# Attention 1 of a graph network: 20 destination blocks instead of 16 leave the gathers, the windows are sought before the table, and the run table comes in as an input

## The chip, the core and the metric

The kernel runs on one core of a Trainium2 chip. The metric is device time in microseconds (us) for one execution. The kernel before takes 4396.92 us, the median of three runs (4395.07 to 4397.64).

The core has five engines that run side by side, each from its own in-order queue: PE (matmul; PEld is its weight load), DVE (vector), ACT (scalar, activation), POOL (GpSimd) and SP (it only issues DMAs here). DMAs are issued from the queues of SP, ACT and POOL. Gathers of table rows by index (indirect DMAs) are issued from POOL's queue. SBUF is the working memory of 128 partitions, PSUM holds matmul results, and tensors named `dram` lie in HBM.

## The reference, cut to what matters

Input are 6250 nodes of 128 features and 200000 edges `src -> dst`, sorted by `dst`. Two graph layers follow each other, each behind a layer norm and a ReLU, each added to its input:

```
h = relu(layernorm(x))
x = x + gat(gat(h, 4 heads of 16).elu(), 1 head of 128)   # attention 1, attention 2
h = relu(layernorm(x))
x = x + conv(h)                                           # edge MLP, messages, scatter-add

gat: feat = x @ W;  el, er = (feat * attn_l).sum, (feat * attn_r).sum
     e = leaky_relu(el[src] + er[dst]);  alpha = softmax of e over the edges of one dst
     out[dst] = sum of alpha * feat[src]
```

The change lies in attention 1: for each destination node, the softmax-weighted sum of the features of its edges' sources, with four heads.

## The kernel before, in words

Nodes are taken in NB = 49 blocks of 128. The program has four stages: a head (layer norm, features, the table), attention 1, attention 2, and the convolution.

**Head.** `x` is loaded in seven pieces. `norm_stats` (L289) makes mean and variance of a block. The loop at L574 takes four blocks at a time: ReLU of the normed rows on ACT (L579), transposes on PE, an eviction on DVE (L314), a matmul with the weights (L591), and evictions into `t1` (L593) and `er1` (L594). `t1` is written to the HBM tensor `table1` in four parts (L600): 76 words a node, being features, `el` and two exponentials of it. Beside this, the first edge of each block is sought in the sorted `dst` (L205 to L241): compare with the first entry of segments of 40, sum the counts by matmul, fetch one segment a block, and count in it. `write_runs` (L258) writes a table `runs` of overlapping runs of 128 edges (`src` and `dst` as 16-bit words, one run every 16 edges).

**Attention 1, gathered blocks.** NG = 49 - DENSE1 = 33 blocks are gathered. A window of 34 x 128 edges is loaded for each. The edges come in five groups (8, 8, 8, 8 and 2 tiles of 128 edges, `GROUPS`). `gather` (L317) issues one indirect DMA a tile, so 34 a block, into one of six buffers `G`. `attend` (L353) makes a one-hot of the destinations (L324), the node factors by matmul (L360 to L366), the messages (L367), splits them in two halves (L331, L332), and adds them up by matmul (L377). `load_low` (L342) loads, for each block, the low bits of `dst` to all partitions (`oht`, 1088 KB), and `node_hot` (L350) makes a one-hot of it. `finish1` (L793) ends four blocks: division by the sums, ELU, and the rows for attention 2.

**Counts.** Attention 2, and the dense blocks of attention 1, need for each pair of source and destination node how many edges join them. These counts are made for all 49 blocks, in 196 steps of a quarter block. A window of two destination nodes holds at most 128 edges. `seek_windows` (L710) looks for the first edge of each window, 25 chunks of 128 windows: a first search by compares and matmuls stands at L617 to L627; then, for each chunk, one indirect fetch of a segment of 160 entries (L715) and a count in it (L720, L721). `fetch_run` (L729) fetches the runs by index, `cut_windows` (L736) turns them to keys, and `count` (L764) compares them with all slots (two instructions at L773), multiplies (L784), casts on ACT (L786), and writes the counts to HBM (L788).

**Attention 1, dense blocks.** The last DENSE1 = 16 blocks are not gathered. `dense1` (L852) takes four blocks at a time, in two passes of two heads, and runs over all 49 source blocks in seven steps of seven: load counts and factors (L861, L864), a steep ReLU on ACT that says for each pair of nodes on which side of the leaky ReLU it lies (L892), its minimum with the counts on DVE (L895, one instruction for each of two heads, 112 in all), and matmuls (L902, L908). `fill_rhs1` (L684) makes the factors from the table in seven steps, each with multiplications and splits at L694 to L705.

**Order.** The loop at L1003 goes over the gathered blocks and their groups. It mixes in count steps and dense steps by how far it has come: count steps from block LAG = 3, dense steps from block LAG_D = 7, both spread to the end of the last gathered block (L1027, L1030). The fetches of the segments (L715) go between the gathers of the first two blocks and the rest at the start of the third, the fills stand in the second and third. A framework orders the instructions of each engine around this and sets the semaphores; `keep` fixes the order of those that are wrapped in it. After the loop, flags are made (miscounts, overflow) and branched on, and attention 2 begins.

**Attention 2** takes two blocks at a time over all 49 source blocks: counts loaded, a ramp on ACT (L1188), two instructions on DVE (L1192, L1193), matmuls (L1197). **The convolution** takes the edges in 1563 tiles with one gather each.

Of the kernel before, what the change touches and what calls it, by code (L numbers as in the profile page):

```python
# [42 lines left out]
P = 128  # L43
SB = 8
GROUPS = ((0, 8), (8, 8), (16, 8), (24, 8), (32, 2))
K = 34
# [7 lines left out]
LAG = 3  # L54
AHEAD = 4
DENSE1, LAG_D = 16, 7
# [10 lines left out]
def gnn_kernel(ctx: ExitStack, tc: tile.TileContext, x, src, dst, attr4, attr8,  # L67
               W1, al1, ar1, b1, W2, al2, ar2, b2,
               Wl0, Wl1, Ws0, Ws1, Wm1, Wm2, Wtp, Wf0, Wf1, src_t, dst_t, attr4_t, attr8_t, out):
# [23 lines left out]
    NROW = (E - WCAP) // WSTEP + 1  # L93
# [11 lines left out]
    ps_bank = ps_pre.enter_context(tc.tile_pool(name="ps_bank", bufs=2, space=PSUM))  # L105

# [52 lines left out]
    fin = one.enter_context(tc.tile_pool(name="fin1", bufs=1))  # L159
    aw = one.enter_context(tc.tile_pool(name="aw", bufs=2))  # L160
# [3 lines left out]
    df = seek.enter_context(tc.tile_pool(name="df", bufs=1)).tile([GP, ROWT + 1], F32, name="df")  # L164
    listed = ExitStack()
    find = listed.enter_context(tc.tile_pool(name="find", bufs=1))
    both = []
    for name, v in (("di", dst), ("si", src)):
        t = find.tile([GP, ROWT + WCAP], I32, name=name)
        nc.vector.memset(t[:, ROWT:], NB * P)  # L170
        rows = v.rearrange("(p t) -> p t", p=GP)
        nc.sync.dma_start(t[:, :ROWT], rows)
        nc.sync.dma_start(t[:GP - 1, ROWT:], rows[1:, :WCAP])
        both.insert(0, t)

    w1_sb = const.tile([D, HD], F32, name="w1_sb")
    nc.scalar.dma_start(w1_sb, W1)
    load_x()
    w2_sb = const.tile([HD, D], F32, name="w2_sb")
    nc.scalar.dma_start(w2_sb, W2)  # L180
    a1_sb = const.tile([HD, 2 * H1], F32, name="a1_sb")
    nc.vector.memset(a1_sb, 0.0)
    for j, a in ((0, al1), (1, ar1)):
        for h in range(H1):
            nc.scalar.dma_start(a1_sb[h * DH:(h + 1) * DH, j * H1 + h:j * H1 + h + 1],
                                a[h:h + 1, :].rearrange("o d -> d o"))
    a2_sb = const.tile([D, 2], F32, name="a2_sb")
    for j, a in ((0, al2), (1, ar2)):
        nc.scalar.dma_start(a2_sb[:, j:j + 1], a.rearrange("o d -> d o"))
# [5 lines left out]
    wfirst = const.tile([P, NC], I32, name="wfirst")  # L195

    runs = dram.tile([NROW, 2, WCAP], I16, name="runs")
    di = both[1]
    nc.vector.tensor_copy(df, di[:, :ROWT + 1])
    falls = find.tile([GP, ROWT], F32, tag="row", name="falls")  # L200
    nc.vector.tensor_tensor(falls, df[:, :ROWT], df[:, 1:], op=OP.is_gt)
    fall = find.tile([GP, 1], F32, name="fall")
    nc.vector.tensor_reduce(fall, falls, axis=AX.X, op=OP.max)
    NS = ROWT // SEG
    below = find.tile([GP, NB + 1, NS], F32, name="below")  # L205
    nc.vector.tensor_tensor(below, df[:, 0:ROWT:SEG][:, None, :].to_broadcast([GP, NB + 1, NS]),
                            starts[:GP, :, None].to_broadcast([GP, NB + 1, NS]), op=OP.is_lt)
    nbelow = find.tile([GP, NB + 1], F32, name="nbelow")
    nc.vector.tensor_reduce(nbelow, below, axis=AX.X, op=OP.add)
    ps = small()  # L210
    nc.tensor.matmul(ps[:NB + 1, 0:1], nbelow, ones[:GP], start=True, stop=True)
    nc.tensor.matmul(ps[:NB + 1, 1:2], fall.to_broadcast([GP, NB + 1]), ones[:GP], start=True, stop=True)
    seg = find.tile([NB + 1, 1], F32, name="seg")
    nc.vector.tensor_scalar(seg, ps[:NB + 1, 0:1], -1.0, 0.0, op0=OP.add, op1=OP.max)
    seg_i = find.tile([NB + 1, 1], I32, name="seg_i")
    nc.vector.tensor_copy(seg_i, seg)
    part_i = find.tile([NB + 1, SEG], I32, name="part_i")
    nc.gpsimd.indirect_dma_start(
        out=part_i, out_offset=None, in_=dst.rearrange("(s t) -> s t", t=SEG),
        in_offset=bass.IndirectOffsetOnAxis(ap=seg_i[:, 0:1], axis=0))  # L220
    part = find.tile([NB + 1, SEG], F32, name="part")
    nc.vector.tensor_copy(part, part_i)
    nc.vector.tensor_scalar(part, part, own_start[:NB + 1], None, op0=OP.is_lt)
    found = find.tile([NB + 1, 2], F32, name="found")
    nc.vector.tensor_reduce(found[:, 1:2], part, axis=AX.X, op=OP.add)
    nc.vector.scalar_tensor_tensor(found[:, 0:1], seg, float(SEG), found[:, 1:2], op0=OP.mult, op1=OP.add)
    nc.vector.tensor_copy(found[:, 1:2], ps[:NB + 1, 1:2])
    pr = small()
    for j in range(2):
        nc.tensor.matmul(pr[:1, j * P:j * P + NB + 1], found[:, j:j + 1], ident[:NB + 1, :NB + 1],  # L230
                         start=True, stop=True)
    ends = find.tile([1, 2, NB + 1], F32, name="ends")
    nc.vector.tensor_copy(ends, pr[:1, :2 * P].rearrange("o (j b) -> o j b", j=2)[:, :, :NB + 1])
    first = find.tile([1, NB], F32, name="first")
    nc.vector.tensor_scalar(first, ends[:, 0, :NB], float(E - CAP), None, op0=OP.min)
    nc.vector.tensor_copy(first_i, first)
# [9 lines left out]
    for t in both:  # L246
        raw = pool.tile([P, LONG], BF16, tag="row", name="raw", bufs=3)[:GP, :ROWT + WCAP].bitcast(I16)
        nc.scalar.copy(raw, t)
        raws.append(raw)
# [1298 lines left out]
```

## Time and profile before

| what | value |
|---|---|
| runs, median of three | 4396.92 us |
| the profiled execution | 4406.11 us, span 4404.4 us |
| before the first gather of attention 1 | 112.7 us |
| first to last gather of attention 1 | 112.68 to 1778.53 us |
| last gather to the first ramp of attention 2 | 1778.53 to 1849.45 us |
| attention 2, then convolution, to the end | 1849.45 to 4404.4 us |
| busy over the span: PE, DVE, ACT, POOL | 69%, 81%, 62%, 63% |
| mean granted PE clock | 0.832 |

A profile is one execution of the kernel; its times are from the start of its span. The page has, for each engine, the busy share of 40 equal slices of the span as digits (9 is 90% or more). A group of instructions shows the line, the engine, the operation, what is written from what, and how often; then the busy time, the mean length of one in ns, and the idle time of the engine just before them with what ended it. "issue" there means that the engine waited for nothing the profile shows. The timeline lists instructions by start and length. A line of waits reads: who waited for whom, us in total, how many times, the longest. SPq, ACTq are the DMA issues in those queues.

### The profile page before, as it was taken

The numbers are of one execution on the slowest core, as the hardware profiler recorded it, in microseconds if no ns is written. First come the engines' busy times: TensorE is split into PE (matmuls) and PEld (weight loads), VectorE is DVE, ScalarE is ACT, GpSimd is POOL, SyncE is SP. The second block draws the span as 40 slices with busy tenths as digits, with TensorE's granted clock in tenths as the row PEclk, the third lists the DMA queues.
The fourth block names the chain that finished last, engine by engine and source line by source line (L and its number), as shares of the span: only waits on it lengthen the run. The fifth ranks groups of instructions, "written<-read, shape, count | busy, mean of one in ns | idle before, by whom it ended". The sixth has DMA issues, their size and how long they took to land. (4 is left out here: it accounts for less than half of the span.)

```text
span 4404.4 us, 61759 instructions
## 1 busy us (share of the span) xinstructions
PE 3042.9 (69%) x19255; PEld 2147.9 (49%) x19256; DVE 3565.2 (81%) x6184; ACT 2712.6 (62%) x6200; POOL 2795.3 (63%) x2752
## 2 busy tenths in 40 slices
PE   4115665666477566579998677777777777777777
PEld 3115444544355444478887344444444444444444
DVE  5258776788688688688888799999999999899998
ACT  3024556576486577689999565555555555555555
POOL 0777777777777777110000777777777777777775
PEclk9999677677677778699999788888888888888888
DMA  4346464565466556554453222222222222222221
GB/s 109 67 120 171 128 168 129 164 177 158 126 178 165 150 156 169 172 177 167 153 171 107 61 63 63 62 63 64 62 63 63 63 62 63 63 62 63 64 61 51
DMA packets 410029, 484.00 MB, mean 110 GB/s; under 512 B 248457, under 2 KB 296367, under 8 KB 405454
## 3 DMA queue, kind: packets, MB, share of 16 engines
q1 hardware_dynamic: 258854, 239.58, 18.6%
q0 software_dynamic: 87952, 149.96, 15.0%
q10 hardware_dynamic: 62872, 90.28, 5.7%
q8 instruction: 159, 2.61, 0.3%
q14 instruction: 192, 1.57, 0.1%
HBM read 369.70 MB, written 109.82 MB: 109 GB/s over the span
## 5 line engine op out<-in xcount | busy, mean ns | idle before, releaser
L319 POOL DMA_INDIRECT G<-table,srcc x1563 | 1475.1, 944 | 1003.3 <-DVE kept L1239 525.6
L319 POOL DMA_INDIRECT G<-table,srcw x1122 | 1249.0, 1113 | 417.1 <-issue 314.9
L786 ACT CAST ca<-small 128x392 bf16<-128x392 f32 x784 | 350.2, 491 | 335.9 <-PE small L784 307.0
L892 ACT ACTIVATE up<-erb,sel 128x512 bf16<-128x512 f32 x784 | 516.1, 726 | 8.6 <-DMA oht<-dlow 3.6
L1188 ACT ACTIVATE ramp<-erb,sel 128x256 bf16<-128x256 f32 (+1 forms) x1225 | 491.7, 499 | 20.7 <-DVE up L1192 14.4
L1335 PE MATMUL whole<-halves,ohr 128*128 128x512 f32 x1563 | 503.9, 461 | 0.7 <-ACT acc L1365 0.7
L1277 ACT ACTIVATE g<-G,a 128x128 f32<-128x128 f32 x1563 | 481.4, 393 | 2.0 <-DMA G<-table,srcc 0.2
L1270 PEld LDWEIGHTS big<-wtp_sb,hid 64*128 64x128 f32 x3126 | 263.6, 249 | 372.8 <-issue 358.2
L1270 PE MATMUL big<-wtp_sb,hid 64*128 64x128 f32 x3126 | 306.1, 351 | 150.2 <-DVE halves L1324 149.8
L784 PE MATMUL small<-key,lo 128*128 128x98 bf16 x3136 | 299.9, 237 | 139.6 <-ACT ca L786 109.0
L908 PE MATMUL up<-up,rc 128*102 128x512 bf16 x784 | 297.0, 539 | 142.2 <-DVE up L895 141.4
L1335 PEld LDWEIGHTS whole<-halves,ohr 128*128 128x128 f32 x1563 | 316.6, 210 | 129.5 <-issue 54.1
L377 PE MATMUL whole<-halves,ohr 128*128 128x136 f32 x1122 | 240.1, 356 | 174.6 <-DVE halves L332 138.7
L1258 PE MATMUL layer<-hid,wm_sb 128*128 128x512 f32 x392 | 341.1, 969 | 11.9 <-ACT hid L1261 11.1
L1261 ACT ACTIVATE hid<-layer 128x512 f32<-128x512 f32 x392 | 230.8, 589 | 189.6 <-PE layer L1258 189.6
L1258 PE MATMUL layer<-a8t,wm_sb 16*128 16x512 f32 x392 | 230.0, 667 | 157.2 <-ACT hid L1261 148.1
L784 PEld LDWEIGHTS <-lo 128*128 128x128 bf16 x3136 | 228.7, 115 | 209.9 <-issue 175.9
L1315 ACT CAST halves<-mess 128x512 fp32r<-128x512 f32 x195 | 114.4, 587 | 329.7 <-DVE mess L1302 329.7
L1307 DVE TENSOR_TENSOR halves<-mess,halves 128x512 fp32r<-128x512 f32 x391 | 267.8, 685 | 55.3 <-ACT halves L1310 39.8
L377 PEld LDWEIGHTS whole<-halves,ohr 128*128 128x128 f32 x1122 | 204.7, 255 | 194.7 <-DVE halves L332 137.3
L1197 PE MATMUL big<-rhs,up 128*128 128x196 bf16 x2401 | 240.5, 250 | 49.6 <-DVE up L1192 41.6
L773 DVE TENSOR_TENSOR lo<-slots,turned 128x2048 bf16<-128x2048 bf16 x196 | 238.3, 1216 | 37.4 <-PE small L784 37.2
(296 smaller groups left out, 6294.4 us busy)
## 6 DMA issues: line engine op xcount, KB each, us to landing
counts<-ca ACTq DMA_DIRECT2D x196, 392.0 KB
ct<-counts SPq DMA_DIRECT2D x192, 392.0 KB
ctc<-counts SPq DMA_DIRECT2D x896, 56.0 KB
oht<-dlow SPq DMA_DIRECT2D x33, 1088.0 KB
G<-table,srcc POOLq DMA_INDIRECT x1563
rc<-rhs SPq DMA_DIRECT2D x56, 358.8 KB
G<-table,srcw POOLq DMA_INDIRECT x1122
a8t<-attr_rows SPq DMA_DIRECT2D x391, 16.0 KB
```

The source lines that it names most:

```text
L319: nc.gpsimd.indirect_dma_start(out=G[:, c, :], out_offset=None, in_=table, in_offset=bass.IndirectOffsetOnAxis(ap=idx[:, c:c + 1], axis=0))
L377: nc.tensor.matmul(acc, oh[:, c, :], ms[:, c].rearrange("e s f -> e (s f)"), start=start and c == 0, stop=stop and c == n - 1)
L784: nc.tensor.matmul(ps[:, k * NKEY:(k + 1) * NKEY], lo[:, a, :, r], ky[:, a, :, r], start=True, stop=True)
L786: nc.scalar.copy(ca[:, :, i * W:(i + WBANK) * W].rearrange("p h (k d) -> p h k d", d=W), ps[:, :WBANK * NKEY].rearrange("p (k h d) -> p h ...
L892: nc.scalar.activation(up[:, i], erb[:, j], AF.Relu, bias=sel1[:, h0 + i, 2 * q + j:2 * q + j + 1], scale=STEEP)
L908: nc.tensor.matmul(sums["ups"][j][:2 * C1, :], r[:, i, c:c + 2 * C1], up[:, i], start=h0 + i == 0, stop=h0 + i == NB - 1)
L1188: nc.scalar.activation(ramp[:, h, :n * P], erb[:, :n * P], AF.Relu, bias=sel2[:, h0 + h, :], scale=STEEP)
L1258: keep(nc.tensor.matmul(ph, w, x[:, :npr * P], start=True, stop=True))
L1270: keep(nc.tensor.matmul(pw[:, c, :], hid[half, j * P:(j + 1) * P], wtp_sb[half].rearrange("x p u -> x (p u)"), start=True, stop=True))
L1277: keep(nc.scalar.activation(g0[:, c], G[:, c, :], AF.Copy, scale=a0[:, c, :]))
L1307: keep(nc.vector.tensor_tensor(ms[:, cs, 1, 1], m, ms[:, cs, 0, 1], op=OP.subtract))
L1335: keep(nc.tensor.matmul(acc, oh[:, c, :], ms[:, c].rearrange("e s h i u -> e (s h i u)"), start=start, stop=stop))
```

## The change

It does five things.

1. DENSE1 goes from 16 to 20: 29 blocks are gathered, 20 are dense. The dense steps start at block 3 and are due 20 tiles before the end of the last gathered block; the count steps start at block 0 and are due three blocks before it.
2. `runs` is an input of the program in 32-bit words; `write_runs` and the load of `src` for it are gone. So are most small weight loads: `a1_w`, `a2_w`, `lin_w`, `wm1_w`, `wm2_w`, `wtp_w` and `wf_w` come in ready-made and are loaded whole, on SP.
3. The search for the windows goes ahead of the table: the compares (`segments`), the fetches in five groups of five chunks (`fetch_parts`) and the counts in them (`count_parts`).
4. The head is written as a pipeline in a kept order: statistics of eight blocks at a time, `features` in five phases of which each call of `through` advances up to five groups of blocks, with the eviction of the transposes on ACT. The table is written in three parts of 24, 16 and 9 blocks. The check whether `dst` falls (`find_falls`) comes last.
5. The pools `fin1` and `aw` are opened once the memory of the head is released, the fills stand in blocks 0 and 1, and statistics and the windows' shift have a kept order.

```diff
-LAG = 3
 AHEAD = 4
-DENSE1, LAG_D = 16, 7
+DENSE1, LAG_D, AFTER, AFTER_D = 20, 3, 3, 20
...
+    def segments(i0, i1):
+        for i in range(i0, i1):
+            below = find.tile([GP, NC * P], BF16, name="belowc", bufs=2)
+            keep(nc.vector.tensor_scalar(below, wstarts, df[:, i * WSEG:i * WSEG + 1], None, op0=OP.is_gt))
+            for c in range(NC):
+                keep(nc.tensor.matmul(pcount[:, c:c + 1], below[:, c * P:(c + 1) * P], ones_b, start=i + c == 0,
+                                      stop=i == NSEG - 1 and c == NC - 1))
...
+    def fetch_parts(q):
+        part = find.tile([P, NQS, WSEG], I32, name="wpart_i", bufs=2)
+        for j in range(NQS):
+            nc.gpsimd.indirect_dma_start(
+                out=part[:, j, :], out_offset=None, in_=dst.rearrange("(s t) -> s t", t=WSEG),
+                in_offset=bass.IndirectOffsetOnAxis(ap=wseg_i[:, q * NQS + j:q * NQS + j + 1], axis=0))
+        wparts[q] = part
+
+    def count_parts(q):
+        less = find.tile([P, NQS, WSEG], F32, name="wpart")
+        cs = slice(q * NQS, (q + 1) * NQS)
+        keep(nc.vector.tensor_tensor(less, wparts.pop(q), own_w[:, cs, None].to_broadcast([P, NQS, WSEG]), op=OP.is_lt))
+        keep(nc.vector.tensor_reduce(wfound[:, cs], less, axis=AX.X, op=OP.add))
...
+    def through(k):
+        for d in range(5):
+            if 0 <= k - d < len(gens):
+                next(gens[k - d])
+
+    c0 = stats(0)
+    keep(nc.vector.tensor_copy(df, di))
+    deque(c0, 0)
+    c1 = stats(1)
+    through(0)
+    segments(0, 1)
...
+    segments(6, NSEG)
+    window_segments()
+    for q in range(2):
+        fetch_parts(q)
...
+    through(9)
+    write_table(0, 24)
+    through(10)
+    count_parts(1)
+    fetch_parts(3)
+    through(11)
+    through(12)
+    count_parts(2)
+    fetch_parts(4)
+    through(13)
+    write_table(24, 40)
+    through(14)
+    through(15)
+    through(16)
+    write_table(40, NB)
     pq = pool.tile([P, NB, 2 * H1], F32, name="pq")
     node_factors(pq, er1, H1)
     split3(pre, pq3, pq, [P, NB, 2 * H1])
+    for q in range(3, 5):
+        count_parts(q)
+    window_rows()
...
     for b in range(AHEAD):
         load_window(b)
+    for c in chunks[:2]:
+        fetch_run(c)
     for b in range(AHEAD):
         shift_window(b)
     low = load_low(0)
+    tables[chunks[0]] = cut_windows(chunks[0])
     for b in range(NG):
-        if b == LAG - 1:
-            deque(seeking, 0)
-        if b == LAG:
-            tables[chunks[0]] = cut_windows(chunks[0])
...
-            if b < LAG - 1:
-                for _ in range(2):
-                    next(seeking, None)
-            if b + 1 < LAG:
-                write_runs(b * len(GROUPS) + q, (LAG - 1) * len(GROUPS))
-            if b == 1 or b == 2 and q < NB // HS - len(GROUPS):
-                fill_rhs1(((b - 1) * len(GROUPS) + q) * HS, HS)
-            if b == LAG - 1 and q == 3:
-                for c in chunks[:2]:
-                    fetch_run(c)
-            due = len(steps) * ((b - LAG) * K + s + n) // ((NG - LAG) * K)
+            if b == 0 or b == 1 and q < NB // HS - len(GROUPS):
+                fill_rhs1((b * len(GROUPS) + q) * HS, HS)
+            due = min(len(steps), len(steps) * (b * K + s + n) // ((NG - AFTER) * K))
             todo = deque(steps[done:max(done, due)])
             done = max(done, due)
-            due = n_dense * ((b - LAG_D) * K + s + n) // ((NG - LAG_D) * K)
+            due = min(n_dense, n_dense * ((b - LAG_D) * K + s + n) // ((NG - LAG_D) * K - AFTER_D))
             more = max(0, due - taken)
```

## The prediction

> **What bounds the kernel now.** I read the page's slices first. The gathers of attention 1 and of the convolution are the two blocks of POOL work. Attention 1 lasts until about slice 17, and POOL stands at 7 there from slice 2 on.
>
> ```profile
> POOL 0777777777777777110000777777777777777775
> L319 POOL DMA_INDIRECT G<-table,srcw x1122 | 1249.0, 1113 | 417.1 <-issue 314.9
> L892 ACT ACTIVATE up<-erb,sel 128x512 bf16<-128x512 f32 x784 | 516.1, 726 | 8.6 <-DMA oht<-dlow 3.6
> ```
>
> A 7 looks like slack, but the idle time in front of the gathers is "issue": POOL waited for nothing. The timeline shows the step, here with the DVE row that lies under it:
>
> ```profile
> 1762.41 0.94 POOL L319 DMA_INDIRECT G<-table,srcw  x1 [0.30 <-issue]
> 1763.66 0.94 POOL L319 DMA_INDIRECT G<-table,srcw  x1 [0.30 <-issue]
> 1764.33 2.01 DVE L895 TENSOR_TENSOR up<-up,ctc 128x3584 bf16<-128x3584 bf16 x1
> 1764.91 2.25 POOL L319 DMA_INDIRECT G<-table,srcw  x1 [0.30 <-issue]
> 1767.46 0.95 POOL L319 DMA_INDIRECT G<-table,srcw  x1 [0.30 <-issue]
> ```
>
> One gather steps every 1.25 us (0.95 busy, 0.30 issue), back to back, except where a dense min (L895) runs: that gather takes 2.25 instead of 0.94. So POOL is the bound of attention 1 at "78%". The table by stretches gives the others' load:
>
> ```profile
> 112.70:300.00 187.30, 23.56 (x162) 21.84 (x161) 61.19 (x194) 13.39 (x27) 141.58 (x146) 1.00 0.37 85
> 300.00:430.00 130.00, 69.69 (x524) 62.18 (x525) 116.28 (x307) 63.52 (x141) 99.68 (x96) 1.00 0.58 161
> 430.00:1779.00 1349.00, 867.67 (x6052) 627.55 (x6050) 1038.21 (x1829) 865.22 (x1725) 1057.44 (x932) 0.73 0.58 157
> 1779.00:1870.00 91.00, 52.63 (x367) 40.66 (x365) 54.83 (x134) 57.21 (x133) 0.00 (x0) 0.66 0.46 163
> ```
>
> Columns: stretch, length, busy PE, PE loads, DVE, ACT, POOL, clock. DVE is 33% busy in the first stretch and 77% in the third. What DVE waits for, between 600 and 1750 us:
>
> ```profile
> DVE w L364 <- DMA G<-table,srcw: 130.4, 27, 9.1
> DVE lo L773 <- PE small L784: 36.9, 34, 3.0
> DVE h L810 <- PE small L807: 18.1, 8, 3.9
> ```
>
> Most of its idle time is waiting for gathered rows. Last, the two ends of the stage:
>
> ```profile
> 72.70 27.42 SPq L600 DMA_DIRECT2D table<-t  x4
> 112.68 0.96 POOL L319 DMA_INDIRECT G<-table,srcw  x1 [65.17 <-PE pe L360]
> 1777.59 0.94 POOL L319 DMA_INDIRECT G<-table,srcw  x1 [0.30 <-issue]
> 1820.44 0.22 ACT L989 COPY sums<-whole 128x68 f32<-128x68 f32 x1
> 1839.11 0.33 ACTq L788 DMA_DIRECT2D counts<-ca  x1
> 1841.77 0.33 SPq L830 DMA_DIRECT2D rhs2d<-rr  x1
> 1849.45 5.69 ACT L1188 ACTIVATE ramp<-erb,sel 128x256 bf16<-128x256 f32 x14
> ```
>
> The last table write is issued by 100.12, the gathers run from 112.68 to 1778.53 (1665.9 us), then 70.9 us pass until attention 2's first ramp: counts and dense work spread to the last gathered block are still being worked off.
>
> **The change, part by part** (in the profiled execution: 4406.1 us, span 4404.4; it lies 9.2 above the median 4396.9, and I carry the difference over).
>
> *Gathers.* 33 blocks become 29: 4x34 = 136 gathers leave the POOL queue, and the 25 fetches of window segments (L715), which stood between the gathers at the same step (122.69, 123.94), go ahead of the first gather. The 25 run fetches stay. 161 x 1.25 = -201.3 us.
>
> *Mins.* A fifth group of four dense blocks brings 28 mins: 112 become 140. Of the 112, 107 start before the last gather; with the dense work due 20 tiles before the end I count all 140 there, 33 more. Price of one: the gathers cost 212.5/211 = 1.007 us before 430, where no min runs, and 1036.5/913 = 1.135 after. Excess over 0.94 after 430: 178 us, at most 178/107 = 1.66 a min; taking off the earlier background (0.067 each, 61 us) leaves 1.09. Samples: 2.25 - 0.94 = 1.31, and 1.39 at 1771.21. I take 1.3, by the samples: +42.9 (36 to 55). Four fewer node one-hots (L350, 1.37 long) give back about 0.8 each: -3.
>
> The Trainium skill, page "SBUF — State Buffer", section "SBUF: two separate sides", says that a DMA issued by GpSimd cannot write its descriptors while VectorE holds the port pair both share, and then blocks to the end of that instruction. The rows agree: the long gather ends 0.8 us behind its min. By the rule a min could cost up to its whole 2.02 us; 33 of them would be 67 in place of 43.
>
> *Gather stage: -161.*
>
> *Head.* Window segments (ten compares of about 1 us and 250 small matmuls, at 100 to 108 before), five groups of fetches and the blocks' firsts now lie ahead of the table's last write, in a kept order. DVE had 62.9 us busy in the first 112.7; the edit adds about 6 there (counts of parts). The 25 fetches (31 us) lie under POOL's 65.17 us idle; without that cover the last five would cost 6. Gone: the load and cast of src (781 KB), and the run writes (625 KB each) which share the queues with the table's landing between 100.12 and 112.68. In ACT's queue 13 evictions of about 0.6 replace DVE's; ACT had 33.3 busy of 112.7. The first two run fetches stand behind two gathers in POOL's queue and wait for the last counts of parts on DVE, which have falls (1.79 and 1.81) and the factors' split (about 2) in front of them; the other gathers queue behind that wait. It is covered by the table's landing, 12.6, or costs up to 5 of it. That 12.6 can shrink to the 7.6 that a 1088 KB load takes (issued 50.64, used 58.26); kept order on in-order engines can cost as much as the ten compares. I take -6, between -20 and +15. The kept weights' loads move to SP ahead of the windows; nothing waits for them until later.
>
> *Compute beside the gathers.* Counts run from block 0, due three blocks early: 196/26 = 7.54 steps a block (was 196/30 = 6.53); mins 140 over 864 tiles, 5.51 a block (was 112/26 = 4.31). DVE rows: a gathered block 16.5 (four groups of 1.21+0.72+0.68+0.35+0.22+0.18, a small one, the one-hot 1.37), a count step 1.216+0.963 = 2.18, a min 2.02, the rest 4.2. Before: 16.5+14.2+8.7+4.2 = 43.6; measured between 600 and 1750 (790 gathers, 23.2 blocks of 49.5): busy 38.2, waiting for gathered rows 6.0, other waits 5.3. So rows overlap by a factor 0.876. After: 16.5+16.4+11.1+4.6 = 48.6, busy 42.6, other waits 5.9: 48.5 us. POOL's block: 34x1.25 + 1.2 (run) + 5.51x1.3 + 1.5 (the one-hot's 0.8 and small delays) = 52.4. POOL stays the bound, by 3.9 us. ACT by the same scaling 38.5, PE 37.1. Blocks 0 and 1 also hold the seven fills (L694 to L705, 49.5 us of DVE): about 60 a block against POOL's 45, a lag of 30; POOL runs ahead by six buffers of eight tiles, 60 us, which hides it. If that cover is gone the lag falls on the path. I take +10 (0 to 70).
>
> *Tail.* With counts due three blocks and the dense work 20 tiles early, behind the last gather stand: landing 2.5, the last small group 5 (sum of its DVE and ACT rows), finish1 6.5 (1820.44 to 1826.95), flags and branch 11 (1838.48 to 1849.45): 25, and a little lag: 30. 30 - 70.9 = -41 (-11 if DVE is still a block behind).
>
> Attention 2 and the convolution keep their work; the statistics now have a kept order in attention 2 too, hidden behind ACT, which is busy 512.1 of the 530 us from 1870 to 2400 (without that cover, the 12 groups could cost about 1 us each); runs as an input of 32-bit words makes a fetch 1 KB a row, which no row prices, and the fetch is a POOL step like any other (1043 ns against 1113): zero, at most 25x1.
>
> **Sum:** -161 - 6 + 10 - 41 = -198: 4406.1 - 198 = 4208 in the profiled execution, **4199 us** by the median.
>
> **The rivals.**
> - *Compute becomes the bound of the first 26 blocks.* For it: DVE would be 42.6/52.4 = 81% busy there (77% before), PE 71% at a granted clock of 0.73. Against: 1700 to 1800 held DVE at 87.5% and the gathers still stepped on. If the other waits double to 12 a block, a block takes 42.6 + 12 = 54.6: 2.2 more in 26 blocks, 57, and some 10 of lag are left at the tail: about 4265.
> - *The tail stays*: work due early is done late, since every engine queue is in order. +30: 4229.
> - *The mins cost the gathers their whole length*: 33 x 0.7 more, 4222. This is the skill's rule at its end.
> - *Slower.* The node one-hots' load (oht, 1088 KB) stands in SP's queue among 16 loads of counts per dense step; SP waited 309 us there for mins to free buffers. If it is exposed in each block, 29 x 7.6 = 220 come back: 4419. It decides from 7 us a block; between 600 and 1750 DVE waited for it 4.3 us in 23 blocks.
>
> **How the numbers follow.** Forecast 0.52 (its own range 4170 to 4225), compute bound 0.20, tail 0.12, long mins 0.10, slower 0.05, else 0.01. Low end: head -20, mins at 1.09, no drag, tail 25: -235, 4160. High end takes in the compute bound: 4285. Within 0.2% is 8.8 us, about what a measurement can tell from no change; only a near full loss lands there (0.01). Faster 0.94, slower 0.05.
>
> **What would show it.** In the profile after: 986 gathers of about 1.14 to 1.16 us, idle still "issue", none behind DVE; the first near 106, the last near 1610; 30 us to the first ramp; attention 2 and convolution as long as before (2555 us from the first ramp to the end). Wrong if gathers wait for "DVE msg" or "PE pe", if DVE's waits for gathered rows vanish while a block is longer than 53, or if the first gather comes after 125.

## The result, and the profile after

The changed kernel takes 4268.82 us, the median of four runs (4261.89 to 4277.34), against 4397.28 us for the kernel before beside it (four runs, 4395.07 to 4398.40). The ratio is 0.9709, 95% interval 0.969 to 0.9728: 128.5 us faster. The forecast was 4199, so a third of the expected gain did not come, and the time lies close to the rival in which compute becomes the bound (4265).

The profiled execution took 4266.29 us (span 4264.5). Its parts beside those of the kernel before, from the timelines of the two:

| part | before | after | difference | forecast |
|---|---|---|---|---|
| start to the first gather | 112.7 | 114.4 | +1.8 | -6 |
| first to last gather | 1665.9 | 1542.2 | -123.7 | -161 + 10 |
| last gather to the first ramp | 70.9 | 50.4 | -20.5 | -41 |
| first ramp to the end | 2554.9 | 2557.5 | +2.6 | 0 |

The sum is -139.8; the profiled execution of the kernel before lay 9.2 us above its median, that of the changed one 2.5 below.

The stage of the gathers can be taken apart further. A POOL step of 1.25 us (0.94 busy, 0.30 issue) is one unit; what a gather or fetch takes above 0.94 is its excess; a gap between two steps above 0.45 us, less the usual 0.30, is a wait. Issues after the first gather: 1172 became 1011, x 1.25 = -201.3. Excess: 193.4 became 225.1, +31.7. Waits: 10.2 (in 3 gaps) became 55.8 (in 18 gaps), +45.6. Together -124.0, which is the measured -123.7.

The page of the changed kernel, slices and groups:

```profile
POOL 3777777777777774100003777777777777777775
L346 POOL DMA_INDIRECT G<-table,srcw x986 | 1149.5, 1166 | 362.6 <-issue 269.0
...
L945 DVE TENSOR_TENSOR up<-up,ctc 128x3584 bf16<-128x3584 bf16 x140 | 282.8, 2021 | 68.2 <-ACT up L942 56.6
```

The gathers' block of 7s is about one slice shorter, and their mean went from 1113 to 1166 ns, because more of them lie under a min (L945). The mins themselves are as long as before (2021 ns), but 56.6 us of idle time now stand in front of them, waiting for the activations L942 (before, 15.8 us in front of L895).

The two ends of the stage, from the timelines of POOL and ACT, with a step under a min (2.29 us long) between them:

```profile
114.45 0.94 POOL L346 DMA_INDIRECT G<-table,srcw  x1 [6.42 <-PE small L713]
...
1651.87 2.29 POOL L346 DMA_INDIRECT G<-table,srcw  x1 [0.30 <-issue]
...
1655.72 0.94 POOL L346 DMA_INDIRECT G<-table,srcw  x1 [0.30 <-issue]
...
1707.05 1.31 ACT L1228 ACTIVATE ramp<-erb,sel 128x256 bf16<-128x256 f32 x3
```

The step is what it was, 1.25 us, and 2.29 for 0.94 under a min (L945 at 1651.33).

What POOL waited for between the first gather and the last (us in total, times, longest):

```profile
POOL G L346 <- issue: 269.0, 882, 0.3
POOL G L346 <- DVE w L389: 41.4, 15, 10.8
POOL G L346 <- DVE msg L394: 13.3, 9, 4.1
POOL G L346 <- DVE w L391: 11.1, 10, 4.4
```

882 gathers still start 0.3 us behind the one before with nothing to wait for. Nearly all of the rest is new (before, the gathers waited 13.2 us for `msg` on DVE): L389, L391 and L394 are a group's work on DVE, and L394 is the last to read the buffer of rows. The reading is that POOL had run through its six buffers and stood until DVE had come further. The first such gap is at 649.75 us, the largest is 10.8 us.

The same side of it from DVE, 600 to 1600 us:

```profile
DVE up L945 <- ACT up L942: 53.8, 40, 4.1
DVE lo L823 <- PE small L834: 51.5, 42, 2.9
DVE w L391 <- DMA G<-table,srcw: 12.0, 2, 8.6
```

Before, from 600 to 1750 us, DVE waited 130.4 us for gathered rows and 36.9 for the counts' matmuls (L784, now L834). Now it hardly waits for rows; it waits for ACT and PE. Busy times by stretch (length, PE, PE loads, DVE, ACT, POOL, clock, DMA share, GB/s):

```profile
430.00:1657.00 1227.00, 832.64 (x5752) 582.88 (x5751) 990.99 (x1689) 906.72 (x1769) 931.76 (x785) 0.77 0.61 167
1657.00:1707.00 50.00, 16.38 (x77) 12.61 (x76) 23.40 (x115) 9.18 (x28) 0.00 (x0) 0.55 0.18 45
```

DVE is 81% busy (77% before), ACT 74% (64%), PE 68% (64%). No engine is full, and yet POOL is held up. The last row is the tail: 50 us without a gather, with DVE busy for 23.4. What fills its second half shows in DVE's timeline:

```profile
1682.38 0.18 DVE L533 CAST flag_i<-flag 1x50 int32<-1x50 f32 x1
...
1683.93 0.30 DVE L879 TENSOR_TENSOR rr<-x,rr 128x130 bf16<-128x130 f32 x1 [0.36 <-ACT rr L878]
1684.14 0.43 DVE L313 TENSOR_SCALAR dstw<-dsti 128x34 f32<-128x34 int32 x4
1687.24 0.18 DVE L313 TENSOR_SCALAR dstw<-dsti 128x34 f32<-128x34 int32 x1 [2.66 <-DMA dsti<-in_dst]
...
1703.94 0.27 DVE L313 TENSOR_SCALAR dstw<-dsti 128x34 f32<-128x34 int32 x2 [3.54 <-DVEq L503]
```

The last real work of attention 1 ends at 1684.2 and the flags are made at 1682.6. Then come 20 us of `shift_window` (L313) for the windows of the dense blocks, one for each load of a window, about 1.3 us apart. No instruction reads these windows, because dense blocks are not gathered.

### The profile page after: what moved, and what is told of

Read it like the earlier page. It is cut to its first block, busy times and chain, and to the rows that moved or that the text cites. A ratio compares the mean times of both kernels' runs of the same rounds, so it can differ in the third digit from the quotient of the medians.

```text
span 4264.5 us, 62159 instructions
## 1 busy us (share of the span) xinstructions
PE 3058.5 (72%) x19331; PEld 2133.9 (50%) x19332; DVE 3570.7 (84%) x6078; ACT 2829.5 (66%) x6395; POOL 2703.0 (63%) x2616
## 3 DMA queue, kind: packets, MB, share of 16 engines
q1 hardware_dynamic: 293108, 252.64, 20.5%
## 5 line engine op out<-in xcount | busy, mean ns | idle before, releaser
L346 POOL DMA_INDIRECT G<-table,srcw x986 | 1149.5, 1166 | 362.6 <-issue 269.0
L942 ACT ACTIVATE up<-erb,sel 128x512 bf16<-128x512 f32 x980 | 637.0, 723 | 11.8 <-DMA counts<-ca 5.9
L958 PE MATMUL up<-up,rc 128*102 128x512 bf16 x980 | 342.7, 507 | 148.6 <-DVE up L945 148.4
L834 PE MATMUL small<-key,lo 128*128 128x98 bf16 x3136 | 295.4, 233 | 129.8 <-ACT ca L836 97.8
L1373 PEld LDWEIGHTS whole<-halves,ohr 128*128 128x128 f32 x1563 | 317.0, 210 | 132.4 <-issue 58.5
L945 DVE TENSOR_TENSOR up<-up,ctc 128x3584 bf16<-128x3584 bf16 x140 | 282.8, 2021 | 68.2 <-ACT up L942 56.6
L834 PEld LDWEIGHTS <-lo 128*128 128x128 bf16 x3136 | 227.9, 113 | 211.6 <-issue 157.5
L958 PEld LDWEIGHTS <-rc 128*102 128x102 bf16 x980 | 157.9, 165 | 265.3 <-issue 234.4
```

Of the source, the lines that this page charges most:

```text
L346: nc.gpsimd.indirect_dma_start(out=G[:, c, :], out_offset=None, in_=table, in_offset=bass.IndirectOffsetOnAxis(ap=idx[:, c:c + 1], axis=0))
L834: nc.tensor.matmul(ps[:, k * NKEY:(k + 1) * NKEY], lo[:, a, :, r], ky[:, a, :, r], start=True, stop=True)
L942: nc.scalar.activation(up[:, i], erb[:, j], AF.Relu, bias=sel1[:, h0 + i, 2 * q + j:2 * q + j + 1], scale=STEEP)
L958: nc.tensor.matmul(sums["ups"][j][:2 * C1, :], r[:, i, c:c + 2 * C1], up[:, i], start=h0 + i == 0, stop=h0 + i == NB - 1)
L1373: keep(nc.tensor.matmul(acc, oh[:, c, :], ms[:, c].rearrange("e s h i u -> e (s h i u)"), start=start, stop=stop))
```

## The experiments

All are edits of the changed kernel unless said otherwise. The parts of each one's profiled execution, us (issues after the first gather; excess and waits as above; the last column is the ratio of its time to the kernel before beside it):

| kernel | median | first gather | gather stage | issues | excess | waits | last gather to ramp | ratio, 95% |
|---|---|---|---|---|---|---|---|---|
| before | 4397.28 | 112.7 | 1665.9 | 1172 | 193.4 | 10.2 | 70.9 | 1 |
| after | 4268.82 | 114.4 | 1542.2 | 1011 | 225.1 | 55.8 | 50.4 | 0.9709 (0.969 to 0.9728) |
| free shift | 4256.81 | 114.4 | 1550.7 | 1011 | 209.8 | 79.7 | 33.5 | 0.9672 (0.9654 to 0.969) |
| no dead windows | 4252.10 | 113.9 | 1547.1 | 1011 | 219.5 | 66.4 | 34.2 | 0.9657 (0.9638 to 0.9677) |
| after, 16 dense | 4347.42 | 114.5 | 1627.3 | 1147 | 196.2 | 0.0 | 41.2 | 0.9885 (0.9868 to 0.9901) |
| before, 20 dense | 4369.51 | 112.8 | 1594.7 | 1036 | 205.4 | 96.7 | 105.5 | 0.993 (0.9914 to 0.9947) |
| half the gathers | 4183.19 (one run) | 113.5 | 1409.2 | 547 | 134.8 | 592.6 | 100.3 | - |
| mins split in 7 | 4258.30 | 113.4 | 1538.2 | 1011 | 141.8 | 133.6 | 48.3 | 0.9684 (0.9668 to 0.97) |
| mins late | 4267.26 | 114.4 | 1540.8 | 1011 | 224.0 | 55.7 | 49.3 | 0.9707 (0.9689 to 0.9725) |
| head | 4264.97 | 112.2 | 1541.5 | 1011 | 220.8 | 59.6 | 51.4 | 0.9702 (0.9686 to 0.9719) |
| combined | 4229.94 | 112.0 | 1516.7 | 1011 | 130.8 | 124.8 | 41.8 | 0.9614 (0.9601 to 0.9627) |

### The tail: the shift of the windows without its kept order

```diff
-        keep(nc.vector.tensor_scalar(dstw[:, b, :], raw_dst.pop(b), -float(b * P), None, op0=OP.add))
+        nc.vector.tensor_scalar(dstw[:, b, :], raw_dst.pop(b), -float(b * P), None, op0=OP.add)
```

> The changed kernel, with only the shift of the windows (L313) no longer in a kept order. Theory: the 20 us behind the last real work of attention 1 (rhs2d written at 1682, first ramp of attention 2 at 1707) are the shifts of the dense blocks' windows, which the kept order holds behind everything else on DVE, each with its window's loads in front. Free, they move up among the gathers: the stretch from the last gather to the first ramp falls from 50 to about 30 us, time about 4249. Rival: the windows' loads are a chain of their own in SP's queue, or the stretch has another cause: still 50 us, about 4269.

The stretch from the last gather to the first ramp fell from 50.4 to 33.5 us. The time fell less (ratio 0.9672 against 0.9709, 16 us), since the gather stage of this execution is 8.5 us longer, with 24 us more of waits. So the kept order was what made the tail long; the two ratios' intervals only touch, and the stretch itself is from one execution of each.

### The tail: the windows of the dense blocks dropped

```diff
-        if b + AHEAD < NB:
+        if b + AHEAD < NG:
             load_window(b + AHEAD)
-        if b:
+        if b and b + AHEAD - 1 < NG:
             shift_window(b + AHEAD - 1)
...
-    for b in range(NG + AHEAD - 1, NB):
-        if b >= NG + AHEAD:
-            load_window(b)
-        shift_window(b)
```

> The changed kernel, without the windows of the 20 dense blocks (loads L308, L310 and shift L313 for blocks 29 to 48, which no later instruction reads). Theory as for the free shift: 50 us become 30, about 4249, and here neither loads nor shifts can be left in the way. If the stretch stays at 50, what holds attention 2 back is another thing.

34.2 us, and a time 23 us lower by the ratios. In DVE's timeline of this kernel nothing is left between the last rows of attention 1 and the next stage but the branch:

```profile
1688.64 0.30 DVE L879 TENSOR_TENSOR rr<-x,rr 128x130 bf16<-128x130 f32 x1 [0.37 <-ACT rr L878]
1693.04 0.17 DVE L150 MEMSET xt<- 128x128 f32 x1 [4.11 <-DVEq L503]
```

From the last gather (end 1661.0) to 1688.9 is 28 us of work, then 4 of the branch and 2 to the ramp. The forecast's 30 was right for what it counted.

### The change taken apart: 16 dense blocks in the new kernel, 20 in the old

```diff
-DENSE1, LAG_D, AFTER, AFTER_D = 20, 3, 3, 20
+DENSE1, LAG_D, AFTER, AFTER_D = 16, 4, 3, 20
```

> The changed kernel with 16 dense blocks instead of 20 (33 gathered; dense steps from block 4, since the counts that they need are made by then). Theory (POOL's steps set the gather stage, with some 45 us of waits for the others): 136 gathers x 1.25 = +170, 28 mins x 1.24 = -35, most of the waits gone -40, four windows fewer at the end -4: about +91, 4360. Rival (DVE sets the stage from 650 us on): four blocks of DVE work +66, 28 mins x 2.02 = -57: +9, about 4278.

and, in the kernel before,

```diff
-DENSE1, LAG_D = 16, 7
+DENSE1, LAG_D = 20, 7
```

> The kernel before with 20 dense blocks and nothing else changed (dense steps still from block 7, counts from block 3, segment fetches among the gathers, run table written by the kernel). Theory (POOL's steps): 136 x 1.25 = -170, 28 mins x 1.24 = +35: -135 at best, 4262; the dense steps are crowded into 22 blocks (6.4 mins a block), so waits of POOL like those of the changed kernel (45) or more: about 4300 (4262 to 4330). Rival: the gain of the change is mainly the moved search and the counts from block 0, and more dense blocks alone make DVE the limit: 4370 or more.

The first came out at 4347, nearer to POOL's side (4360) than to DVE's (4278); its waits are gone altogether:

```profile
POOL G L346 <- issue: 306.4, 1005, 0.3
```

The second missed by 70 us, and hit the rival's 4370. The kernel before with 20 dense blocks waits more than the changed one:

```profile
POOL G L319 <- issue: 265.3, 870, 0.3
...
POOL G L319 <- DVE w L362: 63.4, 17, 10.8
POOL G L319 <- DVE msg L367: 37.6, 14, 13.1
```

Against their own runs of the kernel before (4400.5), the four more dense blocks alone give 31 us and all the rest of the change alone gives 53. Together they give 128.5, so some 44 us are had only together. Without the rest of the change, POOL waits 96.7 instead of 55.8 us, and the tail takes 105.5 instead of 50.4. A reason that fits is that counts from block 0 and dense steps from block 3 make the room on DVE, ACT and PE that the fifth group of dense blocks needs; no run moves these starts alone.

The rest of the change by itself, between before and 16 dense after: 25 issues x 1.25 = -31.3, waits -10.2, excess +2.8: -38.7, which is the stage's -38.6. The dense blocks, between 16 and 20 in the new kernel: 136 x 1.25 = -170, excess +28.9, waits +55.8: -85.3 against a stage shorter by 85.1.

### How much the other engines need by themselves: half of the gathers left out

```diff
-        G = gath.tile([P, SB, R1], F32, tag="G", name="G")
-        gather(G, table1, srcw[:, b, s:s + n], n)
+        if s // SB % 2 == 0:
+            kept1["G"] = gath.tile([P, SB, R1], F32, tag="G", name="G")
+            gather(kept1["G"], table1, srcw[:, b, s:s + n], n)
+        G = kept1["G"]
```

> The changed kernel, with the gathers of the second and fourth group of each block left out (464 of 986): these groups compute on the rows of the group before, so attention 1 gets wrong sums; all other work stays. It shows what the engines beside POOL need for the stage when POOL is not in the way (POOL: 547 issues x 1.25 = 684 us and at most 174 for the mins). DVE was busy 253 us up to 430 and 991 us from there: 1244 of the 1542 us of the stage. Theory (POOL sets the pace, the others are close behind): DVE's 1244 plus its other waits, 5.9 us a block by the prediction's rows, some 150: about 1400, 140 less. Rival A (POOL alone is the limit, DVE's waits vanish with it): about 1250. Rival B (the others have been the limit since 650 us): only the stretch before 650 shrinks, by at most 100: 1440 or more.

The stage took 1409 us, as expected, but the expectation was too simple: POOL finishes early and the other engines work on for 100 us behind the last gather. From the first gather to the first ramp are 1509.5 us, against 1592.6 in the changed kernel. So 83 us are what taking half of the gathers out of the way gives (the windows at the end are in both). Now POOL mostly waits:

```profile
POOL G L346 <- DVE msg L394: 357.2, 28, 27.7
POOL G L346 <- issue: 132.3, 433, 0.6
POOL G L346 <- DVE w L389: 127.8, 17, 34.9
```

So POOL without any wait would need 1542.2 - 55.8 = 1486 us and 50 of tail, 1537; the others, with POOL out of the way, need 1509; both together need 1593. The two limits lie 2% apart, and together they cost 56 us more than the longer one.

Where the 83 us were gained says which limit holds where. There are 145 groups of gathered tiles, and L394 makes the messages of each. From the first group's messages to the 50th's, the changed kernel takes 543 us and this one 483; from the 50th's to the 120th's, 755 and 751; over the last 25 groups, 242 and 223. The middle of the stage goes at the same pace in both, though in one POOL has half of the gathers. Here are 740 us of each, the changed kernel first, with much the same work on PE, DVE and ACT:

```profile
690.00:1430.00 740.00, 511.47 (x3603) 355.78 (x3601) 620.90 (x1069) 550.84 (x1084) 563.77 (x474) 0.78 0.63 174
624.00:1364.00 740.00, 520.23 (x3608) 361.14 (x3607) 625.27 (x1079) 555.21 (x1093) 316.93 (x257) 0.77 0.56 164
```

So up to about 650 us POOL's steps set the pace, and leaving gathers out gains 60 us there. In the middle DVE, ACT and PE set it, as the expectation's rival B had it, and the last groups, for which the counts are already made, gain another 19. The theory's 1400 us to the last gather was met, but not by its mechanism.

### The mins in seven instructions

```diff
-                    nc.vector.tensor_tensor(by_part, by_part, ct.rearrange("p k a h d -> p h (k a) d"), op=OP.min)
+                    cp = ct.rearrange("p k a h d -> p h (k a) d")
+                    for i in range(HS):
+                        nc.vector.tensor_tensor(by_part[:, i:i + 1], by_part[:, i:i + 1], cp[:, i:i + 1], op=OP.min)
```

> The changed kernel, with each min (L945, 128x3584, 2.02 us) split into seven instructions of 128x512. Theory (a gather's descriptors wait for the end of the DVE instruction that runs, and get in between two): the long gathers shrink, from 1.24 us over 0.94 to at most 0.4 a min, 140 x 0.85 = -119 on POOL, of which the others, which are close behind, leave a half; DVE pays some 0.06 for each of 840 more instructions, 50 us. Together -20 to -70, 4200 to 4250. Rival (seven instructions in a row hold POOL off as long as one): the excess stays at 174 us or grows with DVE's time; DVE's 50 us come on top where it is the limit: 4270 to 4320.

The direction is the theory's, the gain is not (4200 to 4250 were expected). All excess of the gathers together fell by 83 us, 0.60 a min, and the waits rose by 78; a min that runs while POOL waits delays no gather, so a small part of the fall can be that. How much of the rest lies under the mins depends on the count. If each gather's excess is put down to the DVE instruction that overlaps it most, the mins' part fell from some 175 us (1.25 a min) to 42 (0.30); if all gathers that any piece overlaps are counted, it fell from 189 to 110 (0.8). The seven pieces were also not run in a row: the framework put other instructions between them, and only 390 of the 840 pairs of neighbours stayed together.

```profile
POOL G L346 <- issue: 253.5, 831, 0.3
POOL G L346 <- DVE msg L394: 110.9, 24, 21.5
```

POOL then stood longer, for DVE had 36 us more to do (1027.1 busy against 991.0 from 430 us on). The ratio is 11 us better than that of the changed kernel, with overlapping intervals.

### The mins one step later

```diff
+                    def least(by_part=by_part, ct=ct):
                         nc.vector.tensor_tensor(by_part, by_part, ct.rearrange("p k a h d -> p h (k a) d"), op=OP.min)
...
-                    yield [add]
+                    yield [lambda least=least, add=add: (least(), add)[1]]
...
-        while late:
-            late.popleft()()
+        rest = [late.popleft()() for _ in range(len(late))]
+        late.extend(f for f in rest if f)
         late.extend(new)
```

> The changed kernel, with each min (L945) written out one step later than the seven activations (L942, 5.1 us) that it waits for, and its matmuls one step later still; no work is added. Between 600 and 1600 us DVE waited 53.8 us for these activations. Theory (POOL's 56 us of waits come from DVE and PE, held up by such waits in their in-order queues): DVE's wait for L942 falls below 10 us, POOL's waits from 56 to about 20, the stage by 35: about 4235. Rival (the waits come from the sum of work, or another wait takes its place): L942 goes, the stage stays within 10 us: 4260 to 4275.

Nothing moved, and the experiment tells nothing of the theory: the framework orders DVE's instructions itself, and put nearly all of the 140 mins within one place of where they had been. DVE's waits for L942 between 600 and 1600 us stayed, 51.9 us. Whether a later place of the mins would shorten the waits was not tried further.

### The head

```diff
     count_parts(1)
     fetch_parts(3)
+    find_falls()
+    w2_sb, a2_sb = load_weights(("w2_sb", W2), ("a2_sb", a2_w))
+    pw = small()
+    keep(nc.tensor.transpose(pw[:D, :HD], w2_sb, ident[:HD, :HD]))
...
     wide1 = widely(pool, t1[:, :, HD:HD + H1])
-    find_falls()
-    w2_sb, a2_sb = load_weights(("w2_sb", W2), ("a2_sb", a2_w))
...
         oht = node_hot(low)
+        if b == NG // 2:
+            keep(nc.vector.tensor_scalar(wtp_sb[:, 0:3, :], wtp_sb[:, 0:3, :], 1.0 / math.sqrt(HID), None, op0=OP.mult))
...
```

> The changed kernel with three small moves in the head: the check for falls (L279, L281) and the weights of attention 2's scores (L709 to L715) stand right behind the second counts of parts, and the scaling of wtp_sb (L739, L740), which held DVE for 6.6 us at 20 us, is made in the middle of attention 1. Theory: the first gather (114.45) waited for the release of the head's memory behind these; it starts when the last segment fetch (107.73) and the table's last landing allow, near 109: -5, about 4264. Rival: the table's landing (last part issued by 103.1) is the end anyway: 113 or later, no change.

The first gather came 2.2 us sooner, not 5; the time cannot be told from that of the changed kernel. In POOL's timeline the wait has another name:

```profile
103.95 0.94 POOL L223 DMA_INDIRECT wpart_i<-in_dst,wseg_i  x1 [0.30 <-issue]
112.20 0.94 POOL L346 DMA_INDIRECT G<-table,srcw  x1 [7.30 <-DVE wfound L235]
```

L235 is the first instruction behind the last counts of parts, which still stand behind the factors and their split on DVE and read the head's memory too. The table had landed by 112.2 at the latest.

### Due at the end, and 24 dense blocks

```diff
-DENSE1, LAG_D, AFTER, AFTER_D = 20, 3, 3, 20
+DENSE1, LAG_D, AFTER, AFTER_D = 20, 3, 0, 0
```

> The changed kernel with AFTER and AFTER_D at 0: count steps and dense steps are spread to the end of the last gathered block, as before, and not due three blocks and 20 tiles early. Theory (the work due early is done early, and crowds the other engines in the first 26 blocks): a block holds 6.76 count steps instead of 7.54, 0.78 x 2.18 x 0.876 = 1.5 us less of DVE in each of 26 blocks, so POOL's waits fall from 56 to about 20 us and the stage by 35; the tail grows from 50 to 80 or 90 us: within 15 of the changed kernel, 4255 to 4285. Rival (the engines are late with it anyway, so that due early means nothing): the stage falls and the tail stays at 50 to 55: 4235 to 4250.

```diff
-DENSE1, LAG_D, AFTER, AFTER_D = 20, 3, 3, 20
+DENSE1, LAG_D, AFTER, AFTER_D = 24, 3, 3, 20
```

> The changed kernel with 24 dense blocks (25 gathered). POOL's own sum falls by another 136 x 1.25 = 170, less 28 mins x 1.24 = 35. Theory (with half of the gathers left out, the other engines alone took 1509 us from the first gather to the first ramp, against 1593: they are the next limit, and four more dense blocks give DVE about as much as they take, -66 + 57, but ACT 28 x 5.1 = 142 more): POOL waits for most of what it saves, the stretch from the first gather to the first ramp is 1540 to 1600, time 4215 to 4275. Rival (POOL still sets the pace, as from 16 to 20, which gave 76): 4185 to 4200.

Beside these two ran a combination of four edits, whose diff is shown below:

> The changed kernel with four edits together: the windows of the dense blocks dropped (-17 measured), the three moves in the head (-2 to -4 measured), each min in two instructions of 128x2048 and 128x1536 instead of one, and eight buffers of gathered rows instead of six (in the memory that the dropped windows leave). Theory: a gather under a min waits about half as long, 0.6 instead of 1.24: -85 on POOL, of which the others leave a third, -25, as seven pieces gained 11 net of 35 us more of DVE; two more buffers let POOL run 20 us further ahead, -10: about 4215 (4200 to 4240). Rival (the other engines' sum is the limit, whatever POOL does): only the dropped windows and the head count, 4250.

These three ran on a chip on which the kernel before takes 5527.7 us, with instructions of the usual length but engines that stop for up to 22 us (ACT, in the third) without anything the profile shows to wait for, so their numbers can't be set beside the others. There they took 5438.4, 5425.0 and 5434.1 us (ratios 0.9843, 0.9846 and 0.9866, each within 0.007 either way), equal to each other. Both questions, work due at the end and 24 dense blocks, stay open. The third was run again:

### Four edits together

The windows dropped and the head as above, each min in two instructions, and eight buffers of gathered rows (`srcw` and `dstw` shrink to the gathered blocks, which makes the room):

```diff
+                    cp = ct.rearrange("p k a h d -> p h (k a) d")
+                    for i in (slice(0, 4), slice(4, HS)):
+                        nc.vector.tensor_tensor(by_part[:, i], by_part[:, i], cp[:, i], op=OP.min)
...
-    srcw = pool.tile([P, NB, K], I32, name="srcw")
+    srcw = pool.tile([P, NB - DENSE1, K], I32, name="srcw")
...
-    gath = one.enter_context(tc.tile_pool(name="gath", bufs=6))
+    gath = one.enter_context(tc.tile_pool(name="gath", bufs=8))
```

> The kernel of the run before with the four edits together (windows of the dense blocks dropped, three moves in the head, each min in two instructions, eight buffers of gathered rows), once more, where the engines run undisturbed. Theory: the dropped windows give 17 and the head 2 to 4, as measured; the mins in two parts keep a gather waiting half as long, which takes 85 us off POOL's sum, of which the other engines leave a third; the buffers give 10: about 4215 (4200 to 4240), with POOL's waits for the others above 100 us. Rival (the other engines' sum is the limit, whatever POOL does): only the windows and the head count, 4250.

4229.94 us (five runs, 4227.59 to 4238.52), ratio 0.9614 (0.9601 to 0.9627): faster than both kernels, 42 us below the changed one by the ratios, 19 below the one with the windows dropped. The mins by shape:

```profile
L945 DVE TENSOR_TENSOR up<-up,ctc 128x2048 bf16<-128x2048 bf16 x140 | 170.9, 1221 | 17.5 <-ACT up L940 14.4 <-DMA ctc<-counts 1.2 <-issue 1.1
L945 DVE TENSOR_TENSOR up<-up,ctc 128x1536 bf16<-128x1536 bf16 x140 | 133.4, 953 | 14.9 <-ACT up L940 14.8
```

Two instructions cost DVE 304.3 us by their rows instead of 282.8. The excess fell by 94 us, 0.67 a min, so two parts take as much off the gathers as seven did. By the DVE instruction that overlaps a gather most, the two parts hold the gathers up for 0.48 us a min (67 us in all) instead of 1.25. It does not take other work between the parts: where the two had no other DVE instruction between them and lay over a gather (33 times), the gathers that they overlap lost 0.60 us on average, against 1.37 for a min in one piece (103 times, changed kernel). DVE's idle time in front of the mins fell from 68.2 to 32.4 us; the first part need not wait for all seven activations. The waits rose by 69, and the stage is 25.5 us shorter. Of these edits the shares of the two-part mins and of the buffers were not measured apart.

## Why the prediction was right, and where it was wrong

The side and the range held; the gain was forecast 70 us too large. The forecast's own range, 4170 to 4225, was missed: the time lies inside the whole range because its high end takes in the rival that compute becomes the bound. Two of the forecast's own signs of being wrong came true: gathers wait for `DVE msg` (13.3 us), and DVE's waits for gathered rows all but vanish (12.0 us between 600 and 1600) while a block takes 55.1 us, over the 53 that it named. By the steps of the forecast:

- *Gathers, -201.3.* Right. 161 steps of 1.25 us went, and in the kernel with 16 dense blocks, where POOL waits for nothing, 1147 x 1.25 + 196.2 = 1630 gives its stage of 1627.3.
- *Mins, +42.9, one-hots -3.* The price and the number were nearly right, the sum 8 too large. 139 mins start before the last gather, where 107 did, so 32 more for the 33; but a few of them run while POOL stands waiting, and 30 more delay a gather by over 0.1 us (136, before 106). By the DVE instruction that overlaps a gather most, the mins' excess grew by 37 (1.24 for each of the 30, forecast 1.3) and the one-hots' fell by 3.6. All excess together grew by 31.7.
- *The rule of the Trainium skill* (page "SBUF — State Buffer", section "SBUF: two separate sides") that a GpSimd-issued DMA cannot write its descriptors until the VectorE instruction with the shared port pair ends. The same page of the Trainium skill, section "Who interferes with whom", says that a `tensor_tensor` was not seen to stall a DMA; the min is one, and the gathers wait for it (2.29 us for 0.94), so here the measurement decides. On the rule's kind the runs agree: the min in parts delays the gathers about half as much as in one instruction (the whole excess falls by 94 us with two parts, by 83 with seven). Its upper end, 2.02 a min, did not come, and the rival built on it (4222) fell.
- *Compute beside the gathers, +10.* This is the step that failed most: POOL waits 45.6 us more. It was "POOL stays the bound, by 3.9 us", 52.4 us a block against 48.5. Between 600 and 1600 us the changed kernel issues 617 gathers, 18.1 blocks of 55.1 us. POOL's part was right: without its 55.8 us of waits a block takes it 52.0. DVE's was not: it is busy 45.1 us a block (forecast 42.6) and idle for other reasons than gathered rows for 9.3 (forecast 5.9), together 54.4. So from about 650 us to the last blocks the other engines are the bound, by some 2 us a block, and the run with half of the gathers shows the same pace there. The waits of DVE for ACT and PE, 105 us between 600 and 1600, are the largest of the part that was sized too small.
- *Rival "compute becomes the bound", 4265.* Its mechanism held from about 650 us on: it had a block of 54.6 us, and the measured one is 54.4 by DVE's rows, though with more work (45.1 for 42.6) and less waiting (9.3 for 12). That its time was met so closely is in part luck: of the 58 us by which the sum over the profiled execution was off, 36 are POOL's waits (the rival had 57), and 28 are the head and the tail, of which it had 10 at the tail.
- *Head, -6.* It became +1.8. The forecast had the falls in front of the run fetches; these did not wait (116.94 and 118.19, 0.30 behind the gathers). The first gather itself waited, for the release of the head's memory behind the falls and L713. And "nothing waits for them until later" of the weights was wrong:

```profile
17.93 0.21 DVE L728 COPY slots<-slot_b 128x64 f32<-128x64 f32 x1
...
26.11 0.21 DVE L739 TENSOR_SCALAR wtp_sb<-wtp_sb 128x96 f32<-128x96 f32 x1 [6.60 <-DMA wtp_sb<-wtp_w]
```

  The scaling L739 is in a kept order, but as the timeline reads, that order ties an instruction only to the one written before it on its engine. That is L728, which is not kept and ran at 17.93; so L739 came up with it, and DVE stood 6.6 us for a load, ahead of the statistics of blocks 8 to 15. With it moved (head), the first gather came only 2.2 us sooner, so it was not the head's bound.
- *Tail, -41.* It became -20.5. The work that was counted takes what was forecast (34.2 without the windows, for 30). What was missing is that the windows' shift had become kept, a line of the change that the forecast gave no price: 20 windows that nothing reads, in order behind everything, cost 16 to 23 us. The rival "the tail stays" was half right in time and wrong in its reason.
- *The slower rival* (oht exposed in SP's queue) did not come: DVE waited 5.5 us for oht between 600 and 1600.
- *Attention 2 and the convolution, 0.* +2.6.
- *What was to be seen.* The gathers' mean was to be 1.14 to 1.16 us and is 1.166; their idle time was to be "issue" alone, and 66 us of it is behind DVE; the last gather was to come near 1610 and came at 1656, 8 us of it by the later start and 36 by the waits.

In sum, against -198: mins -8, waits +36, head +8, tail +20, rest +3, which leaves the measured -140. POOL's steps, their number and their price, are right. That POOL stays the bound holds for the first third of the stage and its end, not for the long middle; so the waits were mis-sized (+46 for +10). The tail (-20 for -41) was mis-sized for a reason of its own.

## What to carry to other kernels

When the busiest queue is relieved, compare it with what the others need *without* it, not with their busy share: leaving out half of its work shows that in one run, and comparing the pace stretch by stretch shows where each limit holds. Where the two come within some per cent, as here, cutting one alone gave little (the mins in seven, 11 us), and parts of a change were worth more together than apart. An order that is fixed for one reason also fixes when dead or late work is done: look at each kept instruction for what it stands behind, and at the last 50 us for work that nothing reads.

## What the runs showed that was not expected

The stall of the gathers under the mins does not go by how long the mins keep DVE busy. In one, two and seven instructions (2.02 us; 1.22 and 0.95; 0.42 each) they keep it busy for 282.8, 304.3 and 379.7 us over the 140, and yet the gathers' whole excess is 225.1, 130.8 and 141.8 us. Cutting a min in two, with no work taken away, took as much off as cutting it in seven. (The run with two parts holds three other edits; of these, the dropped windows alone left 219.5 and the head alone 220.8, and the two more buffers were not run alone.)

With DVE at 81%, ACT at 74% and PE at 68%, none of them full, the three together set the pace of the long middle of the stage, where POOL, the bound before, stands waiting: each in-order queue waits for the next in turn (DVE 53.8 us for ACT and 51.5 for PE in 1000).
